# Splitting the fields of a pairwise bilinear kernel: later and spread over the row, with the last subtraction on VectorE

## The chip, the cores and the metric

The kernel runs on one core of a Trainium2 chip. The metric is the device time of one execution in microseconds (us). TensorE is called PE (its weight loads PEld), VectorE DVE, ScalarE ACT, GpSimd POOL and SyncE SP; a "q" behind a name means that engine's instruction queue, from which it also issues transfers.

## The reference

There are 32 fields, a batch of 1024 and an embedding of 128. For each of the 496 pairs of fields (i, j) with i < j, the rows of field i are multiplied by the pair's own 128 x 128 matrix, and the result is multiplied elementwise by field j:

```
v_i = inputs[:, I_IDX, :]
v_j = inputs[:, J_IDX, :]
transformed = jnp.einsum('bpd,ped->bpe', v_i, W)
return transformed * v_j
```

Everything is float32. The output has 1024 x 496 x 128 elements, 260 MB; the inputs are 16.8 MB of fields and 32.5 MB of matrices.

## The kernel before

The pairs are walked row by row: a row is one field i, from 30 down to 0, with j from i + 1 to 31, so row i has 31 - i pairs and the rows become longer toward the end. `pairs` lists them, and `first_q[i]` is the number of row i's first pair. Each pair q has two units u = 2q and 2q + 1, one for each half of the batch (512 columns). The schedule is manual: every engine carries out its instructions in the order in which the Python code issues them.

A pair's product is held in one of four PSUM tiles (`po`). The first 15 pairs (`nq0`) use plain float32 matmuls (L223). From there on the kernel splits each operand into parts that TensorE takes in its fp32r form, and computes a product from three matmuls: `first(u)` issues xh with wh and xl with wl (L226), then ACT scales the PSUM tile (L228); `second(u)`, three units later (`LAG`), adds xd with wd (L237). After a pair's second half DVE multiplies `po` by field j into an output tile `ot` (L247). Four pairs share an output tile of 2 MB, which is stored with one transfer from the ACT queue (L276).

The parts come from two helpers. `split_w(c)` makes wh, wl and wd of two pairs' matrices: one ACT instruction (L136) and three on POOL (L138, L139, L140). `split_x(f, a)` makes the parts of one half of field f, beginning at column a: xh on ACT (L154), xl on POOL (L155 and its scaling L156), and xd, the difference of xh and xl. For fields above NF - 2 - NATIVE - SHARED, which is 9 here, xd is put in the list `later` and issued to DVE up to `XDLAG` = 10 units after the split, but no later than two units past 2 * first_q[f] (L286). For fields 0 to 9 it is a third POOL instruction (L160). The parts of a field lie in `spool`, which has two sets, so field i's set is the one that field i + 2 used.

The calls of both helpers are in the list `todo` with the pair from which each may run and the pair by which it is due. The list is sorted by the due pair. Once per pair (at odd u) the first item that may run is taken, behind the unit's own instructions. A weight split may run five pairs ahead of its due pair, and one becomes free every second pair. The two halves of field i may run from the second pair of row i + 1; since the weight splits that are due earlier go first, they are taken two pairs apart near that row's start.

The matrices come in tiles of eight pairs, 512 KB. `rpool` has three slots for them (`WB` = 3). Odd-numbered tiles from 13 on, and the early tiles, are one transfer on SP (L120), called at a pair that `w_at` lists. Even-numbered tiles from 12 on (`WAPART`) are called when the tile three before has been split completely (for tile 56, tile 54); POOL transfers 112 of their rows (L104) and SP the other 16 (L105), and a small transfer to `mark` follows on POOL a few pairs later (L101). SP carries out its transfers in order, and each waits for its slot to be free. Field 0 has no tile of its own: `load_x(0)`, called at pair 421, takes one of these three slots:

```
if f == 0:
    t = rpool.tile([P, WL, P], F32, tag="w", name="x_0").rearrange("p q e -> p (q e)")
```

The slot is free again when both halves of field 0 have been split. Toward the end, tile 54 is called at pair 409, tile 55 at 429, tile 56 at 433, tile 58 at 441 (when the last split of tile 55 has been issued), tile 57 at 445 and tile 59 at 455. Tile 57's first split is issued at pair 451; the last splits of tiles 55 and 56 at pairs 441 and 449.

Fields 1 to 16 come in four groups of 2 MB (`load_group`, L110) at the pairs of `XAT`. Until a group is loaded its place serves as an output tile, so there are seven output tiles at first, and three from pair 293 on, which is near 440 us.

Of the kernel before, what the change touches and what calls it, by code (L numbers as in the profile page):

```python
# [12 lines left out]
NF = 32  # L13
# [5 lines left out]
OG = 4  # L19
EPS = 2.0**-12  # L20
NATIVE = 5
SHARED = 16
XDLAG = 10
LAG = 3
PB = 4
# [22 lines left out]
def kernel(  # L48
# [99 lines left out]
    def split_x(f, a, u):  # L148

        if a == 0:  # L150
            x_s[f] = [spool.tile([P, BT], F32R, tag=t, name=f"{t}_{f}") for t in ("xh", "xl", "xd")]
        s = slice(a, a + HB)
        h, l, d = [t[:, s] for t in x_s[f]]
        nc.scalar.mul(h, x_sb[f][:, s], 1.0 - 2.0**-13)  # L154
        nc.gpsimd.tensor_tensor(l, x_sb[f][:, s], h.bitcast(F32), ALU.subtract)  # L155
        nc.gpsimd.tensor_scalar(l, l.bitcast(F32), 1.0 / EPS, 1.0, ALU.mult, ALU.mult)  # L156
        if f > NF - 2 - NATIVE - SHARED:
            later.append((min(u + XDLAG, 2 * first_q[f] + LAG - 1), d, h.bitcast(F32), l.bitcast(F32)))
        else:
            nc.gpsimd.tensor_tensor(d, h.bitcast(F32), l.bitcast(F32), ALU.subtract)  # L160
# [3 lines left out]
    first_q = {i: q for q, (i, j) in reversed(list(enumerate(pairs)))}  # L164
# [3 lines left out]
    todo = []  # L168
    for c in range(c0, nchunk):
        todo.append(((c - 3) * WC + 1, max(c * WC, nq0), lambda u, c=c: split_w(c, u)))  # L170
    for i in range(NF - 2 - NATIVE, -1, -1):
        for a in range(0, BT, HB):
            todo.append((first_q[i + 1] + 1 if i < NF - 3 - NATIVE else 2, first_q[i], lambda u, i=i, a=a: split_x(i, a, u)))
    todo.sort(key=lambda t: t[1])

    load_w(0, (0, 1, WL), nc.sync)
# [79 lines left out]
    for u in range(2 * NQ + LAG + SLAG):  # L256
        q = u // 2
        if u < 2 * NQ:
            i, j = pairs[q]
# [60 lines left out]
```

## Time and profile before

| | before |
|---|---|
| runs, median (lowest to highest) | 752.89 us (751.0 to 753.16), three runs |
| profiled execution: own time / span | 754.8 us / 752.9 us |
| mean granted TensorE clock | 0.989 |
| PE / DVE / ACT / POOL busy | 705.0 / 628.6 / 636.3 / 613.4 us |
| read from HBM / written to it | 49.29 MB / 260.05 MB |
| mean rate of the transfers over the span | 412 GB/s |
| xd on DVE (L286) | 32 instructions of 1054 ns |
| xd on POOL (L160) | 20 instructions of 1289 ns |
| xl on POOL (L155, L156) | 52 of about 1300 ns, 52 of 687 ns |
| weight split on POOL (L138, L139, L140) | 241 each of 761, 412 and 740 ns |

The span runs from the first to the last instruction of the profiled execution. The page splits it into 40 slices and gives, for each, how busy the engines and the 16 DMA engines were. The table of waits names, for idle time of an engine, the instruction that waited and the one it waited for. A window is a stretch of the span with the same figures. A line number like L138 is that of the listing above.

### The profile page before, as it was taken

Reading aid. Unit: us, or ns where it says so; the run is one execution under the profiler, and the core shown is the slowest. Engines: PE = TensorE matmul, PEld = TensorE weight load, DVE = VectorE, ACT = ScalarE, POOL = GpSimd, SP = SyncE. Lnnn points to the kernel's source line nnn. Section 1 sums busy time; section 2 is a strip of 40 time slices with the busy share of each in tenths; the row PEclk is TensorE's granted clock in tenths of the full one; section 3 lists DMA queues with packets and bytes.
Section 4 is the critical chain, followed back from the end, with each engine's and each line's share of the span. In section 5 each row is a group of like instructions: output and inputs, shape, how many; then the busy total and the mean of one; then the engine's idle time right before and its main releaser. Section 6 shows DMA issues by size and latency. Waiting matters only on the chain.

```text
span 752.9 us, 10606 instructions
## 1 busy us (share of the span) xinstructions
PE 705.0 (94%) x2946; PEld 551.4 (73%) x2946; DVE 628.6 (83%) x530; ACT 636.3 (85%) x1256; POOL 613.4 (81%) x902
## 2 busy tenths in 40 slices
PE   7999999989999999999999989889999999999994
PEld 3577777777787778777778767668787777777783
DVE  3888999979999999987889878578888888877785
ACT  1298999979999999998899978689999898988893
POOL 1789999988888898898988879678888878797660
PEclk9999999999999999999999999999999999999997
DMA  9999999999999999999999999999999999999988
GB/s 345 423 428 427 428 429 426 430 403 379 411 411 423 426 424 426 423 426 418 422 432 422 425 425 402 424 393 392 422 411 424 396 420 401 416 413 405 420 361 338
DMA packets 32938, 310.03 MB, mean 412 GB/s; under 512 B 5104, under 2 KB 5232, under 8 KB 16752
## 3 DMA queue, kind: packets, MB, share of 16 engines
q10 hardware_dynamic: 19584, 261.10, 82.6%
q1 hardware_dynamic: 8864, 36.77, 12.3%
q0 software_dynamic: 4432, 11.48, 4.2%
q8 instruction: 24, 0.39, 0.2%
q14 instruction: 34, 0.28, 0.1%
HBM read 49.29 MB, written 260.05 MB: 411 GB/s over the span
## 4 chain that ended last, share of the span: by engine, by line
PE 58%; POOL 13%; DMA 13%; DVE 8%; issue 4%; ACT 2%; ACTq 0%; SPq 0%; DVEq 0%; POOLq 0%
PE po L226 37%; PE po L237 18%; DMA out_dram<-ot 10%; DVE ot L247 5%; PE po L223 3%; POOL xl L155 3%; POOL wl L138 3%; POOL xd L160 3%; DMA x_g<-in_xt_dram 2%; DVE xd L286 2%; POOL wd L140 2%; POOL xl L156 1%; ACT po L228 1%; POOL wd L139 1%; DMA x<-in_xt_dram 1%
## 5 line engine op out<-in xcount | busy, mean ns | idle before, releaser
L228 ACT ACTIVATE po<-po 128x512 f32<-128x512 f32 x962 | 554.2, 584 | 81.6 <-PE po L226 66.9
L247 DVE TENSOR_TENSOR ot<-po,x 128x1024 f32<-128x1024 f32 x358 | 432.4, 1222 | 78.3 <-DMA out_dram<-ot 18.3
L226 PE MATMUL po<-xh,wh 128*128 128x512 f32 x962 | 381.0, 396 | 15.5 <-DVE ot L247 14.1
L226 PE MATMUL po<-xl,wl 128*128 128x512 f32 x962 | 377.8, 393 | 13.7 <-POOL wl L138 13.5
L237 PE MATMUL po<-xd,wd 128*128 128x512 f32 x962 | 377.1, 392 | 6.7 <-ACT po L228 3.1
L226 PEld LDWEIGHTS po<-xh,wh 128*128 128x128 f32 x962 | 181.3, 189 | 69.2 <-DVE ot L247 32.2
L138 POOL TENSOR_TENSOR wl<-w,wh 128x256 fp32r<-128x256 f32 x241 | 183.4, 761 | 57.3 <-ACT wh L136 53.1
L226 PEld LDWEIGHTS po<-xl,wl 128*128 128x128 f32 x962 | 181.4, 189 | 55.7 <-POOL wl L138 18.4
L237 PEld LDWEIGHTS po<-xd,wd 128*128 128x128 f32 x962 | 181.3, 189 | 47.5 <-ACT po L228 4.8
L247 DVE TENSOR_TENSOR ot<-po,x_g 128x1024 f32<-128x1024 f32 x136 | 164.9, 1224 | 37.0 <-PE po L237 15.6
L140 POOL TENSOR_TENSOR wd<-wl,wd 128x256 fp32r<-128x256 f32 x241 | 178.3, 740 | 20.1
L139 POOL TENSOR_SCALAR wd<-wh 128x256 fp32r<-128x256 f32 x241 | 99.3, 412 | 20.5
L136 ACT ACTIVATE wh<-w 128x256 fp32r<-128x256 f32 x241 | 98.6, 410 | 7.7 <-DVE ot L247 5.7
L155 POOL TENSOR_TENSOR xl<-x_g,xh 128x512 fp32r<-128x512 f32 x32 | 41.6, 1300 | 2.0 <-ACT xh L154 1.7
L156 POOL TENSOR_SCALAR xl<-xl 128x512 fp32r<-128x512 f32 x52 | 35.7, 687 | 4.6
L155 POOL TENSOR_TENSOR xl<-x,xh 128x512 fp32r<-128x512 f32 x20 | 26.2, 1312 | 15.9 <-ACT xh L154 15.6
L286 DVE TENSOR_TENSOR xd<-xh,xl 128x512 fp32r<-128x512 f32 x32 | 33.7, 1054 | 0.3 <-POOL xl L156 0.3
L223 PE MATMUL po<-x,w 128*128 128x512 f32 x60 | 29.2, 644 | 4.2 <-DMA x<-in_xt_dram 4.2
L160 POOL TENSOR_TENSOR xd<-xh,xl 128x512 fp32r<-128x512 f32 x20 | 25.8, 1289 | 1.7
L223 PEld LDWEIGHTS po<-x,w 128*128 128x128 f32 x60 | 11.9, 204 | 20.7 <-issue 14.6
L154 ACT ACTIVATE xh<-x 128x512 fp32r<-128x512 f32 x20 | 12.3, 624 | 11.6 <-DMA x<-in_xt_dram 11.5
L154 ACT ACTIVATE xh<-x_g 128x512 fp32r<-128x512 f32 x32 | 20.0, 624 | 2.0 <-DMA x_g<-in_xt_dram 2.0
(8 smaller groups left out, 36.5 us busy)
## 6 DMA issues: line engine op xcount, KB each, us to landing
out_dram<-ot ACTq DMA_DIRECT2D x122, 2048.0 KB, 12.7
w<-in_wt_dram SPq DMA_DIRECT2D x36, 512.0 KB, 10.7
w<-in_wt_dram POOLq DMA_DIRECT2D x25, 448.0 KB, 11.6
x_g<-in_xt_dram SPq DMA_DIRECT2D x4, 2048.0 KB, 18.5
x<-in_xt_dram SPq DMA_DIRECT2D x14, 512.0 KB, 9.6
out_dram<-ot ACTq DMA_DIRECT2D x6, 512.0 KB, 8.4
w<-in_wt_dram SPq DMA_DIRECT2D x26, 64.0 KB, 6.2
x<-in_xt_dram ACTq DMA_DIRECT2D x4, 256.0 KB, 5.8
```

The source lines that it names most:

```text
L136: halved[c] = nc.scalar.mul(h, raw, 1.0 - 2.0**-13)
L138: nc.gpsimd.tensor_tensor(l, raw, h.bitcast(F32), ALU.subtract)
L139: nc.gpsimd.tensor_scalar(d, h.bitcast(F32), EPS, 1.0, ALU.mult, ALU.mult)
L140: nc.gpsimd.tensor_tensor(d, l.bitcast(F32), d.bitcast(F32), ALU.subtract)
L155: nc.gpsimd.tensor_tensor(l, x_sb[f][:, s], h.bitcast(F32), ALU.subtract)
L160: nc.gpsimd.tensor_tensor(d, h.bitcast(F32), l.bitcast(F32), ALU.subtract)
L223: nc.tensor.matmul(po[q][:, s], w_raw[q // WL][:, q % WL, :], x_sb[i][:, s], start=True, stop=True)
L226: m = nc.tensor.matmul(po[q][:, s], w_s[c][t][:, r], x_s[i][t][:, s], start=t == 0, stop=t == 1)
L228: scaled[u] = nc.scalar.mul(po[q][:, s], po[q][:, s], 1.0 + EPS)
L237: m = nc.tensor.matmul(po[q][:, s], w_s[q // WC][2][:, r], x_s[i][2][:, s], start=False, stop=True, skip_group_check=True)
L247: taken[q] = nc.vector.tensor_tensor(ots[g][:, k, :], po.pop(q), x_sb[j], ALU.mult)
L286: nc.vector.tensor_tensor(*later.pop(0)[1:], ALU.subtract)
```

## The change

SHARED goes from 16 to 26, so the bound NF - 2 - NATIVE - SHARED goes from 9 to -1, and the xd of every field that is split is issued to DVE. The pair from which the two halves of a field may be split moves: row i + 1 has NF - 2 - i pairs, and the first half may be split from one fifth of the row, the second half from three fifths. The due pairs do not change, nor do the fields 25 and 24, which are split near the kernel's start.

```diff
-SHARED = 16
+SHARED = 26
...
     for i in range(NF - 2 - NATIVE, -1, -1):
         for a in range(0, BT, HB):
-            todo.append((first_q[i + 1] + 1 if i < NF - 3 - NATIVE else 2, first_q[i], lambda u, i=i, a=a: split_x(i, a, u)))
+            at = first_q[i + 1] + (NF - 2 - i) * (1 + 2 * (a > 0)) // 5 + 1 if i < NF - 3 - NATIVE else 2
+            todo.append((at, first_q[i], lambda u, i=i, a=a: split_x(i, a, u)))
```

For field 0, whose preceding row has 30 pairs and begins at pair 435, the halves are split at pairs 442 and 454; before they were split at 436 and 438.

## The prediction

> **What bounds the kernel now.** I read the page's first two parts, then the table of waits, then windows of 10 us, then SP's own waits and the timelines around 675 us. First the page:
>
> ```profile
> PE 705.0 (94%) x2946; PEld 551.4 (73%) x2946; DVE 628.6 (83%) x530; ACT 636.3 (85%) x1256; POOL 613.4 (81%) x902
> ...
> DMA  9999999999999999999999999999999999999988
> GB/s 345 423 428 427 428 429 426 430 403 379 411 411 423 426 424 426 423 426 418 422 432 422 425 425 402 424 393 392 422 411 424 396 420 401 416 413 405 420 361 338
> DMA packets 32938, 310.03 MB, mean 412 GB/s; under 512 B 5104, under 2 KB 5232, under 8 KB 16752
> ```
>
> The transfers bind. They run at 420 to 430 GB/s wherever nothing is amiss, and 310.03 MB at 427 would take 726 us of the 752.9. TensorE is close behind: its matmuls start 0.227 us apart in the timeline near 440 us, so a pair of six costs 1.36 us, while a pair's 512 KB of output and 64 KB of weights cost 0.59 MB / 427 GB/s = 1.38 us. So a stall of an engine costs time only where the transfers run dry behind it, or at the end, where no weights are left to load. The table of waits (microseconds, times, longest) shows both kinds:
>
> ```profile
> DVE ot L247 <- DMA out_dram<-ot: 25.9, 22, 4.2
> PEld po L226 <- POOL wl L138: 18.4, 13, 2.4
> PE po L226 <- DVE ot L247: 14.1, 17, 3.4
> PE po L226 <- POOL wl L138: 13.5, 12, 2.0
> ```
>
> GpSimd's splits stop TensorE 12 times for 13.5 us: by windows of this table, 3.0 us in 130 to 215 us, 4.7 in 320 to 440, 5.8 in 440 to 700, about 1.2 us once in each late row. VectorE waits for stores 25.9 us, 22.8 of it in 440 to 700, where three output tiles are left. Where the transfers do run dry is seen in the windows (busy time and count of each engine, granted clock, DMA share, GB/s):
>
> ```profile
> 130.00:150.00 20.00, 18.97 (x84) 15.17 (x83) 18.35 (x16) 18.16 (x37) 18.46 (x27) 1.00 1.01 428
> 160.00:170.00 10.00, 9.98 (x37) 8.09 (x38) 6.92 (x6) 7.11 (x14) 8.51 (x14) 0.83 0.93 386
> 170.00:180.00 10.00, 10.00 (x46) 8.28 (x45) 9.19 (x9) 9.78 (x21) 8.67 (x13) 1.00 0.97 341
> 500.00:510.00 10.00, 8.84 (x39) 6.89 (x38) 7.50 (x7) 8.54 (x18) 9.38 (x13) 1.00 0.88 368
> 510.00:520.00 10.00, 10.00 (x46) 8.29 (x45) 8.95 (x8) 9.31 (x20) 9.21 (x16) 1.00 1.01 361
> ```
>
> [...] a 512 KB weight transfer lands 10.5 us after its issue in 500 to 712 us, behind queued stores, and after 5.7 us in 165 to 215 us, where stores land in 8.2 instead of 14.0 us (230 to 330 us). [...] here the same subtraction takes 1289 ns on POOL (L160) and 1054 ns on VectorE (L286), so the measured ratio of 1.22 is used. [...]
>
> **The change part by part.** (1) The subtraction xd of fields 0 to 9 leaves POOL: 20 x 1289 ns = 25.8 us. VectorE gains 20 x 1054 ns = 21.1 us, 628.6 + 21.1 = 650 us of 753, two in each of ten rows. In rows 5 to 0 that is 12 x 1.05 = 12.6 us, beside 22.8 us in which VectorE waits for stores. One such store issues up to 1 us late; a store lands about 12.0 us after issue there, some 6 us of it behind the one ahead, so a late store should still find the transfers busy. I take 0; if the cover fails, 12 x (1.05 - 0.9 us, a usual wait for a store in VectorE's timeline after 550 us) is about 2 us and 12.6 the end that nothing supports. No gain is possible from this term alone.
>
> (2) Each field's halves are split at one and three fifths of the preceding row and not two pairs apart at its start. Per two pairs (2.7 us) POOL has one weight split of 761 + 412 + 740 = 1.9 us; a half adds 1300 + 687 (+ 1289) ns = 2.0 (3.3) us, so today two halves in a row put it 1.2 (2.5) us per half behind, and the weight split after them is late. Dealt out, and without xd, one half puts it 1.2 us behind and there are 4 to 12 pairs to recover, so the 13.5 us of stalls on POOL should go, as should ACT's 2.0 us wait for x_g near 350 us. What is late next is the transfers, so this pays only where they ran dry. Against 427 GB/s, 160 to 190 us lost 0.96 + 2.0 + 0.3 = 3.3 us (386, 341 and 413 GB/s): a 2.0 us stall on POOL came just before 160, the clock fell to 0.83 in the first window and few stores were queued. I take 3.0 back. 500 to 520 lost 1.4 + 1.5 us; the one stall of 1.2 us there is taken back, the half-speed clock is not. 580 to 590 (401 GB/s, 0.6 us lost) gives 0.3. Rows 9 to 7 (320 to 440 us) give nothing: a backlog of stores covers their stalls. Sum -4.5 us, bounds -6.5 and -0.5.
>
> (3) In the short rows a clamp holds xd of the second half at two units before the row: VectorE's product 1.22 + xd 1.05 = 2.3 us against the 1.36 us until TensorE wants it, 0.9 us for each of fields 23 to 18, with one xd more for field 23: 6.5 us. PEld and PE waited about 12 us in 36 to 160 us already, on the bursts, and the transfers run at 426 to 430 GB/s there. I take 0 (bounds -1, +1).
>
> (4) **A slot is held longer.** Field 0 lies in one of the three slots of the weights. Its halves are split at pairs 436 and 438 today, at 442 and 454 after. SP's waits in 655 to 680 us show whom the slot goes to:
>
> ```profile
> SPq L120 <- POOL wl L138: 13.2, 2, 8.8
> SPq L105 <- POOL xl L155: 10.9, 1, 10.9
> ```
>
> The second line is weight tile 58 (called at pair 441), which takes field 0's slot when its xl is done; tile 57 (called at 445, first split at 451) is queued behind it on SP and takes tile 55's at 667.72. After the change tile 58 takes tile 55's, field 0 is still in its own, tile 56 is read until pair 449: tile 57 has no slot until the wl of pair 449. ACT runs in order, so its wh for pair 451 blocks all evictions behind it, and TensorE with them. The timelines of ACT and POOL give the events:
>
> ```profile
> 674.38 0.41 ACT L136 ACTIVATE wh<-w 128x256 fp32r<-128x256 f32 x1
> 679.17 0.42 ACT L136 ACTIVATE wh<-w 128x256 fp32r<-128x256 f32 x1 [1.99 <-DMA w<-in_wt_dram]
> ```
>
> ```profile
> 676.30 0.73 POOL L138 TENSOR_TENSOR wl<-w,wh 128x256 fp32r<-128x256 f32 x1
> ```
>
> The wh of 674.38 is that of pair 449. With POOL free its wl ends at 674.4 + 0.4 + 0.8 = 675.6; a weight transfer then lands 10.5 us later (10.3 to 12.0), at 686.1 instead of 679.1. ACT is 6.9 us later than today; today's wait of 2.0 us already reaches TensorE with 0.7, so nothing is left to absorb the rest. By then the stores have drained, so the 2.3 us that TensorE still lost to full tiles after 679 (1.7 of it after 700 us by the waits) disappear, and the rest of the kernel runs at TensorE's pace. Net +4.6 us, bounds 0 and +7.
>
> Sum: -4.5 + 4.6 = +0.1 us. The profiled execution took 754.8 us with a span of 752.9; the median of the runs is 752.89, 1.9 us below it. The difference goes on the median: **753.0 us**.
>
> **The rivals.** (F) Faster: the new slot wait does not bite, because the slots go round otherwise than SP's waits suggest, or the transfer lands early as the stores drain. For it: it rests on one place. Against it: the 10.9 us line and the steady 10.5 us. Then 752.9 - 4.5 = 748.4. (S) Slower: the slot wait of (4) at pair 451, price 4.6 us, decides as soon as part (2) gives back less than 2.3 us, because the slow stretches at 160 and 500 us come from the half clock and from thin queues and not from POOL; then up to 757.5. For it: both stretches follow a drop of the clock, and stalls of the same 1.2 us at 543 and 624 us leave the next store's landing where it was. The 2 us of (1) would add to this side. (N) The dealing is not carried out: one item is taken per odd unit, earliest due first, but weight splits come free only at every other pair, so each half moves by a pair at most; I give this nothing.
>
> **How the numbers follow.** 0.3% is 2.3 us, about what a measurement of this kernel can tell from no change. Forecast, 0.45: own range 750.0 to 755.5, of which 0.06 falls faster, 0.34 within, 0.05 slower. F, 0.30: 0.26 faster, 0.04 within. S, 0.25: 0.24 slower, 0.01 within. That makes 0.32, 0.39 and 0.29. The range 748.0 to 757.5 reaches to both rivals' values; beyond lie S with the cost of (1), and F with all 6.5 us of (2), together under 2 in 10.
>
> **What would show it.** Right: no L160 and 52 of L286; PE's wait on POOL wl under 3 us; no window of 160 to 190 us under 400 GB/s; one ACT wait of about 8 to 9 us on DMA w near 680 us, a dry stretch of transfers after it, and no wait on stores from there to the end. Wrong: no such ACT wait (F); 160 to 180 us as slow as before (S); VectorE's waits for stores gone after 440 us and PE waiting for ot in their place, which would be the cost of (1).

## The result, and the profile after

The change makes the kernel slower: 759.56 us median (758.67 to 761.63, four runs) against 751.94 (750.99 to 753.16, four runs), a ratio of 1.0104 with a 95% interval of 1.0076 to 1.0133. That is 7.6 us more, where no change was forecast. The two profiled executions took 758.67 and 754.8 us, so before's is 2.9 us above its own median: the traces are read here for what happens, the ratios for how much.

Line numbers are one higher after the changed line (L227 is the old L226). First the page of the changed kernel:

```profile
PE 703.2 (93%) x2946; PEld 554.7 (73%) x2946; DVE 636.3 (84%) x550; ACT 632.5 (84%) x1256; POOL 594.3 (79%) x882
...
DMA  9999999999999999999999999999999999997998
GB/s 345 427 424 404 383 427 428 379 400 431 410 414 415 426 422 426 425 423 427 425 423 424 426 423 365 428 424 423 425 419 426 420 419 426 405 406 276 401 427 337
DMA packets 32939, 310.04 MB, mean 410 GB/s; under 512 B 5104, under 2 KB 5232, under 8 KB 16752
```

The work has moved as told: POOL is down 19 us, and VectorE is up 8 us: its xd is now 52 instructions of 867 ns, where it was 32 of 1054. The rate of the transfers has new dips: slices 4 and 5, 8 and 9 (which begin at 57 and at 132 us), and 276 GB/s in the slice that begins at 681 us. A fourth, 365 in slice 25, stands where a wait of 5.8 us for full output tiles has just ended. It is no sign of the loss: two kernels below that are not slower than before, SHARED 26 alone and the one with the short rows put back, show 371 there. The old dip of slice 10 (379) is gone, and so are those of slices 27 and 28 (393 and 392). The table of waits:

```profile
DVE ot L248 <- DMA out_dram<-ot: 25.6, 16, 6.6
PE po L227 <- DVE ot L248: 17.7, 12, 5.8
PE po L238 <- ACT po L229: 9.4, 3, 7.6
PEld po L227 <- POOL xl L156: 7.6, 5, 3.1
PE po L227 <- POOL xl L156: 5.7, 4, 2.7
PE po L238 <- DVE xd L287: 5.8, 5, 1.5
```

TensorE's waits on the weights' wl (13.5 us before) are gone. Waits on a field's xl and xd have grown to 11.5 us together (1.4 before), and there is one of 7.6 us on ACT. Its waits for ot are fewer and longer: twelve of up to 5.8 us instead of seventeen of up to 3.4. The windows of the changed kernel show the first two new dips:

```profile
60.00:70.00 10.00, 10.00 (x45) 8.00 (x43) 9.28 (x9) 9.78 (x20) 8.74 (x12) 1.00 0.98 412
70.00:80.00 10.00, 8.70 (x39) 7.14 (x39) 8.62 (x9) 8.51 (x18) 9.16 (x15) 1.00 0.95 371
80.00:90.00 10.00, 7.86 (x34) 5.88 (x33) 7.94 (x8) 7.25 (x16) 8.25 (x12) 1.00 1.00 364
130.00:140.00 10.00, 8.47 (x37) 6.42 (x36) 9.03 (x8) 7.81 (x17) 9.20 (x14) 1.00 0.98 387
140.00:150.00 10.00, 10.00 (x45) 8.26 (x45) 9.19 (x9) 9.78 (x21) 8.96 (x12) 1.00 0.97 366
```

Before, these five windows moved 424 to 431 GB/s. The third dip is the slot. SP's waits in 650 to 700 us, then the timelines of POOL and ACT:

```profile
SPq L105 <- POOL wl L138: 22.3, 3, 9.8
SPq L120 <- POOL xl L155: 16.8, 1, 16.8
SPq L120 <- POOL wl L138: 10.2, 1, 10.2
```

```profile
673.61 0.73 POOL L138 TENSOR_TENSOR wl<-w,wh 128x256 fp32r<-128x256 f32 x1
```

```profile
672.88 0.41 ACT L136 ACTIVATE wh<-w 128x256 fp32r<-128x256 f32 x1
685.03 0.42 ACT L136 ACTIVATE wh<-w 128x256 fp32r<-128x256 f32 x1 [8.63 <-DMA w<-in_wt_dram]
```

It is now a later weight tile, 59, that waits for field 0's xl (the second line). Tile 57 is the third line: SP issues it at 674.37, just as the wl of 673.61 ends, and it lands about 10.6 us later. ACT stands still for 8.63 us. The wh of 672.88 is that of pair 449, which stood at 674.38 before. So up to this point the traced execution of the changed kernel is 1.5 us ahead, and it ends 4.0 us behind (spans of 756.9 and 752.9 us): between these two executions 5.5 us are lost from here on.

### The profile page after: what moved, and what is told of

The parts are those of the page before. It is cut to its first block, busy times and chain, and to the rows that moved or that the text cites. A ratio compares the mean times of both kernels' runs of the same rounds, so it can differ in the third digit from the quotient of the medians.

```text
span 756.9 us, 10630 instructions
## 1 busy us (share of the span) xinstructions
PE 703.2 (93%) x2946; PEld 554.7 (73%) x2946; DVE 636.3 (84%) x550; ACT 632.5 (84%) x1256; POOL 594.3 (79%) x882
## 4 chain that ended last, share of the span: by engine, by line
PE 76%; DMA 13%; DVE 4%; POOL 3%; issue 2%; ACT 1%; ACTq 0%; DVEq 0%; POOLq 0%
PE po L227 48%; PE po L238 24%; DMA out_dram<-ot 11%; PE po L224 4%; DVE ot L248 3%; DMA w<-in_wt_dram 1%; ACT po L229 1%; DVE xd L287 1%; POOL xl L155 1%; POOL wd L140 1%; DMA x<-in_xt_dram 1%; POOL wl L138 1%; POOL wd L139 0%; POOL xl L156 0%; DVE ot L246 0%
## 5 line engine op out<-in xcount | busy, mean ns | idle before, releaser
L227 PE MATMUL po<-xh,wh 128*128 128x512 f32 x962 | 382.1, 397 | 18.0 <-DVE ot L248 17.7
L227 PE MATMUL po<-xl,wl 128*128 128x512 f32 x962 | 378.1, 393 | 5.7 <-POOL xl L156 5.7
L227 PEld LDWEIGHTS po<-xh,wh 128*128 128x128 f32 x962 | 182.4, 190 | 68.4 <-DVE ot L248 30.5
L227 PEld LDWEIGHTS po<-xl,wl 128*128 128x128 f32 x962 | 182.5, 190 | 44.2 <-POOL xl L156 7.6
L140 POOL TENSOR_TENSOR wd<-wl,wd 128x256 fp32r<-128x256 f32 x241 | 180.6, 749 | 20.1
L139 POOL TENSOR_SCALAR wd<-wh 128x256 fp32r<-128x256 f32 x241 | 102.2, 424 | 20.5
L287 DVE TENSOR_TENSOR xd<-xh,xl 128x512 fp32r<-128x512 f32 x52 | 45.0, 867 | 0.0
L156 POOL TENSOR_SCALAR xl<-xl 128x512 fp32r<-128x512 f32 x52 | 33.1, 636 | 4.6
L154 ACT ACTIVATE xh<-x 128x512 fp32r<-128x512 f32 x20 | 12.3, 625 | 11.5 <-DMA x<-in_xt_dram 11.3
L101 POOL DMA_DIRECT2D mark<-in_xt_dram x26 | 16.6, 637 | 0.0
## 6 DMA issues: line engine op xcount, KB each, us to landing
w<-in_wt_dram POOLq DMA_DIRECT2D x25, 448.0 KB, 11.6
```

What stands on the lines that cost most here:

```text
L139: nc.gpsimd.tensor_scalar(d, h.bitcast(F32), EPS, 1.0, ALU.mult, ALU.mult)
L140: nc.gpsimd.tensor_tensor(d, l.bitcast(F32), d.bitcast(F32), ALU.subtract)
L227: m = nc.tensor.matmul(po[q][:, s], w_s[c][t][:, r], x_s[i][t][:, s], start=t == 0, stop=t == 1)
L287: nc.vector.tensor_tensor(*later.pop(0)[1:], ALU.subtract)
```

## The experiments

Twelve kernels ran in three groups of four, each group against its own runs of the kernel before on the same chip (medians 752.72, 752.27 and 751.10 us; the second group ran on another chip than the other two). Ratios are to those, with the 95% interval in brackets. In the diffs, `D` stands for the change's formula and `E` for the old `first_q[i + 1] + 1`.

**Field 0 put back in the changed kernel.**

```diff
-at = D if i < NF - 3 - NATIVE else 2
+at = (D if i > 0 else E) if i < NF - 3 - NATIVE else 2
```

> The change whole, but field 0 is split at pairs 436 and 438 as before, so weight tile 57 has its slot as before. The change costs 7.6 us by the medians (759.56 against 751.94). Slot theory (tile 57's late slot stops ACT and TensorE): ACT's wait on the weight transfer near 676 us falls from 8.6 to about 2 us and the time falls by 5 to 7 us, to 752.5 to 754.5. Rival, early rows (the second halves of fields 23 to 18 come too late, the transfers run dry in 60 to 160 us and the clock drops): it falls by under 3 us, to 756.5 or more. Rival, xd on VectorE: the same, 756.5 or more.

It took 757.04 us, a ratio of 1.0063 (1.0043 to 1.0083). ACT's wait fell to 1.5 us, but the time by only 0.4% of the kernel, as the rivals and not the slot theory expected. The slot is part of the loss; the rest lies elsewhere.

**Field 0 alone dealt out in the kernel before.**

```diff
-at = E if i < NF - 3 - NATIVE else 2
+at = (D if i == 0 else E) if i < NF - 3 - NATIVE else 2
```

> The kernel before with field 0 alone dealt out (pairs 442 and 454), SHARED 16. Slot theory: 4 to 6 us slower than before (756 to 758), with a wait of 8 to 9 us of ACT on the weight transfer near 677 us and TensorE idle for about 7.6 us. Rivals: within 1.5 us of before, since neither the short rows nor VectorE's xd change.

It took 759.32 us, 1.0109 (1.0072 to 1.0146): the slot by itself costs about 8 us here by the ratio, more than expected. ACT waited 10.2 us for the tile and TensorE 8.6.

**SHARED 26 alone.**

```diff
-SHARED = 16
+SHARED = 26
```

> SHARED 26 alone: xd of all fields on VectorE, halves at the old pairs. Slot theory and early rows: within 2 us of before (750 to 754), since neither is touched; TensorE's waits on POOL wl fall from 13.5 to some 5 us. Rival, xd on VectorE costs the late rows: 3 us or more slower than before (755 or more), with TensorE waiting on ot in rows 5 to 0.

It took 751.22 us, 0.9992 (0.9972 to 1.0011). TensorE's waits on POOL wl fell to 3.0 us and those on ot rose from 14.1 to 20.4 us, and nothing was gained or lost: the rival that VectorE's xd costs the late rows 3 us or more falls. Ending the stalls of the late rows, by itself, is worth nothing that can be measured.

**The dealing alone.** The changed kernel with SHARED 16.

> The dealing alone, SHARED 16: fields 0 to 9 keep xd on POOL. Slot theory plus early rows: as slow as the whole change, 757 to 761, with the ACT wait of 8 to 9 us and the dry stretch of 60 to 90 us. If xd on VectorE carries the loss: 753 or less.

It took 762.01 us, 1.0134 (1.0096 to 1.0172), a little more than expected, with ACT's wait of 9.1 us and transfers at 369 to 373 GB/s in 70 to 90 us. The dealing carries the loss. The interval overlaps that of the whole change, so whether VectorE's xd gives something back here isn't settled by it.

**Short rows put back.** Only fields 17 to 1 are dealt out, with SHARED 26.

```diff
+at = (D if 0 < i < 18 else E) if i < NF - 3 - NATIVE else 2
```

> Dealing only for fields 17 to 1; fields 25 to 18 and field 0 as before, xd of all fields on VectorE. The kernel with field 0 alone put back took 757.04 us, before 752.72, SHARED 26 alone 751.22. Short-rows theory (late second halves of fields 23 to 18 empty the transfers in 60 to 160 us): 750.5 to 752.5, and no window of 60 to 160 us under 420 GB/s. Rival, long rows (TensorE running ahead to full output tiles, long waits, clock at half afterwards): 755 or more.

It took 748.04 us, 0.9944 (0.9917 to 0.9971): faster than before, and better than expected. The page's rates show no dip in the first slices after the start:

```profile
GB/s 347 424 424 428 429 429 427 428 424 424 427 414 423 426 424 423 428 422 423 426 426 427 422 429 371 425 426 424 424 423 425 421 424 424 417 409 415 423 379 342
```

The slices that cover 160 to 200 us, which fell to 379 GB/s before, move 424 or more.

**Short rows alone.** The kernel before, with fields 23 to 18 dealt out (`D if i >= 18 else E`).

> The kernel before with the dealing for fields 23 to 18 alone, SHARED 16, field 0 as before. Short-rows theory: 3 to 5 us slower than before (755.5 to 758). Rival, long rows: within 1.5 us of before.

It took 757.82 us, 1.0077 (1.0047 to 1.0107): the short rows cost some 5.8 us by themselves, by the ratio.

**Tile 57 ahead of tile 58.** The change whole, with field 0 held until pair 454, but tile 58 is called when tile 56 has been split (pair 449), so that tile 57 takes tile 55's slot.

```diff
-if w_next and (XAFTER if w_next[0] == XAFTER + 2 else w_next[0] - WB) in spent:
+if w_next and (w_next[0] - 2 if w_next[0] in (XAFTER + 2, XAFTER + 4) else w_next[0] - WB) in spent:
```

> The change whole, with weight tile 58 called when tile 56 has been split (pair 449) instead of tile 55 (441), so that tile 57, called at 445, takes tile 55's slot at once while field 0 still holds its own. Slot theory: ACT waits 2 us or less for tile 57 and the time is that of the kernel with field 0 put back (757.0, between 755 and 758.5). Rival, it is the late split of field 0 and not the slot: 759 or more.

It took 755.27 us, 1.0032 (1.0014 to 1.0049), with ACT's wait at 1.1 us, as the slot theory expected. Field 0 is split as late as in the change, so it is the slot and not the late split. The share of the slot within the whole change is thus 1.04 - 0.63 = 0.4% by the first experiment and 1.04 - 0.32 = 0.7% by this one, each give or take 0.35; by itself it costs 1.1%. Why the two differ by 0.3% is open.

**TensorE kept busy during the wait.** The kernel with field 0 alone dealt out has 34 more matmuls, whose products are overwritten:

```diff
+if u == 2 * 453 + 1:
+    for _ in range(34):
+        m = nc.tensor.matmul(po[q][:, s], w_s[c][0][:, r], x_s[i][0][:, s], start=True, stop=True)
+        apart(m, scaled.get(u - 1))
```

> The kernel before with field 0 alone dealt out (759.32 us), and 34 more matmuls issued ahead of the second half of pair 453, whose products are overwritten: at 0.22 us each they fill about 7.4 of the 8.6 us in which TensorE stands still for tile 57. Clock theory (half speed follows TensorE's idle time): no half-speed stretch at 680 to 690 us, where it was 10.2 us long with 4.2 us of it after the restart, and 1.5 to 2.5 us faster, 757 to 758. Rival, the half speed has another cause: the stretch stays, and the time is the same or longer, 759.3 to 762.

It took 755.70 us, 1.0048 (1.0029 to 1.0067), against 1.0109 without them, which ran in the first group. Adding 7.4 us of useless matmuls saves 0.6% (0.2 to 1.0), 4.6 us by the ratios and 3.6 by the medians. No half-speed stretch is left at 680 to 690 us, as the clock theory expected, and the gain is larger than it expected. ACT still waits 8.7 us in this trace; it waited 10.2 in the one without, so a part of the difference between the traces can be the shorter wait. Windows of the kernel without them (TensorE's busy time and count first, granted clock, DMA share and rate last):

```profile
680.00:686.00 6.00, 0.00 (x0) 0.00 (x0) 0.00 (x0) 0.94 (x3) 0.48 (x1) 0.50 0.12 48
686.00:690.00 4.00, 3.92 (x9) 3.14 (x10) 1.23 (x1) 3.35 (x7) 3.17 (x6) 0.50 0.47 197
```

and of the kernel with them:

```profile
680.00:686.00 6.00, 6.00 (x28) 4.70 (x27) 0.05 (x1) 2.24 (x5) 1.64 (x3) 1.00 0.31 127
686.00:690.00 4.00, 4.00 (x19) 3.23 (x18) 3.62 (x3) 3.94 (x9) 3.36 (x5) 1.00 0.93 393
```

Without them TensorE restarts at half clock and does 9 matmuls in 4 us instead of 19. The granted clock is 0.50 from 680 to 690 us there, and 1.00 over the same 10 us in the kernel with them.

**Both losses taken out.** Fields 17 to 0 are dealt out (`D if i < 18 else E`), tile 57 comes first, and SHARED is 26.

> Both found losses taken out of the change: dealing for fields 17 to 0 only, and weight tile 57 ahead of tile 58; xd of all fields on VectorE. With field 0 at its old pairs this took 748.04 us, 0.56% under before. Theory (short rows and the slot are the whole loss): 0.3 to 0.8% under before, 746 to 750 us. Rival (dealing field 0 costs something beside the slot): over 751.

It took 747.41 us, 0.9942 (0.9920 to 0.9964): faster than both kernels, and within what was expected if the short rows and the slot are the whole loss.

**The same with SHARED 16.**

> The same with SHARED 16, so that fields 0 to 9 keep xd on GpSimd. If dealing alone ends the late rows' stalls and VectorE's part is worth nothing: within 1 us of the kernel with SHARED 26, 747 to 750. If moving xd matters once the halves are dealt: 1.5 us or more above it, with waits of TensorE on POOL wl in rows 9 to 0.

It took 747.45 us, 0.9946 (0.9918 to 0.9974): the same. TensorE's waits on POOL wl in 320 to 700 us, before and then here:

```profile
PE po L226 <- POOL wl L138: 10.5, 10, 1.2
```

```profile
PE po L227 <- POOL wl L138: 0.5, 1, 0.5
```

Dealing alone ends the stalls of the late rows. With the halves dealt, no difference is measured between the two engines for xd (to about 0.35%).

**Field 23 alone, and fields 22 to 18 alone,** dealt out in the kernel before (`D if i == 23 else E`, `D if 18 <= i < 23 else E`).

> The kernel before with field 23 alone dealt out (its halves at pairs 24 and 26, row 23 begins at pair 28). The fields 23 to 18 together cost 0.77%, 5.8 us. If the first stop carries it (2.7 us without matmuls at 51 us, then 3.4 us at half speed): 2.5 to 4.5 us slower than before, with the half-speed stretch at 53 us. If the five later rows carry it: under 1.5 us slower.

> The kernel before with fields 22 to 18 alone dealt out, field 23 as before. If the first stop of field 23 and its half-speed stretch carry the loss of the short rows: under 2 us slower than before. If stops of about 1 us on xl and xd in each of these rows carry it: 3 us or more slower, and transfers under 400 GB/s in 130 to 160 us.

They took 755.62 us, 1.0062 (1.0042 to 1.0082), and 754.22 us, 1.0032 (1.0013 to 1.0051). Both expectations hold in part: field 23 costs 0.6% and the five others 0.3%; dealt out together they cost 0.8%, which within the intervals is the sum. Windows of the kernel with field 23 alone:

```profile
53.00:57.00 4.00, 1.88 (x7) 1.24 (x7) 0.90 (x2) 1.66 (x4) 3.67 (x6) 1.00 1.00 424
57.00:60.00 3.00, 1.29 (x5) 0.82 (x6) 2.50 (x3) 1.41 (x3) 1.94 (x4) 1.00 0.97 414
60.00:70.00 10.00, 10.00 (x39) 8.05 (x38) 7.52 (x7) 8.04 (x18) 7.52 (x11) 0.83 0.78 329
70.00:80.00 10.00, 8.71 (x39) 6.92 (x38) 8.78 (x9) 8.20 (x18) 8.86 (x12) 1.00 0.96 365
80.00:90.00 10.00, 9.84 (x43) 7.63 (x42) 9.71 (x10) 9.62 (x21) 9.33 (x13) 1.00 1.00 351
```

TensorE starts 12 matmuls in these 7 us, where at 0.227 us from one to the next it has room for 31. The half-speed stretch follows, at 60 us and not at 53 as expected; the transfers drop at the same time and stay low for 30 us. Fields 22 to 18 have their dip later: 397, 395 and 379 GB/s in 130 to 160 us, as expected.

## Why the prediction was wrong, point by point

**Part (1), xd on VectorE, taken at 0: nothing measured speaks against it.** SHARED 26 alone gave -0.08% (-0.28 to +0.11). That run ends the stalls of the late rows as well, for which part (2) took 1.5 us, so the 2 us named for a failing cover are not excluded by it. With the halves dealt, xd on VectorE or on POOL gave 0.9942 and 0.9946.

**Part (2), dealing ends the stalls, taken at -4.5 us: right in size, the source of the gain is open.** In the long rows, where only this part acts, the dealing gave -0.54% without and -0.58% with VectorE's xd, -3.7 us each by the medians, and the stalls on POOL wl are gone. But SHARED 26 alone ends all of them except the early ones and gains nothing. For 160 to 190 us the part took 3.0 us back, from one trace in which the clock fell to half after the stop of 2.02 us on POOL wl. The trace of SHARED 26 alone has the same stop, 2.00 us long, at full clock, and its transfers moved 419, 416 and 406 GB/s there, not 386, 341 and 413. So between these two traces most of that dip goes with the half clock, as rival S said, and not every trace has it.

**Part (3), the short rows, taken at 0 with bounds of 1 us: this step failed.** By itself it measured +5.8 us. Within the change it is more: the kernel with tile 57 first (1.0032) and the one that also has its short rows put back (0.9942) lie 0.9% apart, 6.8 us; with field 0 at its old pairs it is 1.2% (1.0063 and 0.9944), each give or take 0.3. The clamp on xd was seen: TensorE waits 5.8 us on xd. Three things were not. First, the second half's xl is late too. Field 23's is issued two pairs before row 23, and in the changed kernel TensorE stops 2.67 us for it, then again for other fields. Second, the step set against its 6.5 us some 12 us of waits of PEld and PE that were there already. Of those in the table for 36 to 160 us, the matmuls' own are the ones that stop TensorE, and they are few:

```profile
PE po L237 <- DVE xd L286: 1.2, 1, 1.2
PE po L237 <- ACT po L228: 1.2, 1, 1.2
PE po L226 <- DVE ot L247: 1.1, 2, 0.6
PE po L226 <- POOL wl L138: 1.0, 1, 1.0
PE po L226 <- POOL xl L156: 0.2, 1, 0.2
```

That is 4.7 us; the others are waits of weight loads, which overlap the matmuls (551.4 us of weight loads and 705.0 us of matmuls in a span of 752.9). In the changed kernel the matmuls wait 11.6 us there: 5.8 on xd, 0.9 on ACT, and

```profile
PE po L227 <- POOL xl L156: 4.9, 3, 2.7
```

Third, the cover did not hold. The step took a rate of 427 GB/s as proof that stores were queued and a late engine cost nothing. The landing times of stores issued in 55 to 95 us, before and then after, show how much was queued:

```profile
out_dram<-ot ACTq DMA_DIRECT2D x6, 2048.0 KB, 12.9
out_dram<-ot ACTq DMA_DIRECT2D x6, 2048.0 KB, 8.4
```

The difference of 4.5 us is about one store of 2 MB at 427 GB/s (4.9 us), so by this estimate one store was in reserve, and the added stops used it up. Over 44 to 160 us the transfers moved 405 GB/s instead of 428, a shortfall worth 6.2 us. The runs show which fields cost the time; that it went through the emptied queue is read from the traces, and how much of it is the half clock after the first stop is open.

**Part (4), the slot, taken at +4.6 us: right in mechanism, and within the change in size.** The events came as told: no slot for tile 57 until the wl of pair 449, a landing time of 10.6 us, ACT's wait of 8.6 us, TensorE's of 7.6, ACT 5.9 us later than before, and almost no waits for stores from there on (1.8 us from 655 us to the end). That it is 5.9 and not 6.9 us comes mostly from the wl, which ended at 674.3 us and not at 675.6. Within the change the slot measured 0.4 to 0.7%, 3 to 5 us. By itself it measured +8.2 us, of which keeping TensorE busy removed about 4.6, by the ratios. What the sum left out is in "the rest of the kernel runs at TensorE's pace": after the stop that pace is half for some microseconds (in the changed kernel 7 matmuls in 686 to 689 us at a granted clock of 0.51, and 14 in the next 3 us at 1.00).

So the sum had +0.1 us, and the 7.5 us that it lacks are about what the short rows cost within the change. The four parts measured alone come to -0.08 - 0.54 + 0.77 + 1.09 = +1.2%, give or take 0.6, and the whole is 1.04%.

The rivals: F fell, since the wait is there. S named part (4) as the decider if part (2) gave back too little; part (2) gave back what was expected, so S's sign was right for a reason that was not its own. N fell: the second half of field 23 came late enough to stop TensorE. The marks set for the profile were met at the slot and at 160 us, and missed the dip at 60 to 90 us, for which none had been set.

## What to carry to other kernels

Work that is dealt out by a share of the time before it must still keep a fixed lead in the shortest stretch: here three fifths of a row of seven pairs left two pairs, 2.7 us, while xh, xl and xd of one half take 0.6, 2.0 and 0.9 us one after the other. Moving the last reader of a tile moves the release of its slot (tile 57 was issued at 667.72 us before and at 674.37 after), so look up who takes that slot next, on which queue, and what waits behind it in order. A rate of 427 GB/s did not tell how much work was queued behind it; by the estimate above the time from a store's issue to its landing did, 12.9 us before and 8.4 after.

## What the runs showed of the hardware

A stop of TensorE can slow the matmuls behind it. The timeline of the changed kernel, start and duration first:

```profile
53.85 0.65 PE L227 MATMUL po<-xl,wl 128*128 128x512 f32 x1 [2.67 <-POOL xl L156]
54.30 0.63 PE L238 MATMUL po<-xd,wd 128*128 128x512 f32 x1
54.73 0.63 PE L227 MATMUL po<-xh,wh 128*128 128x512 f32 x1
...
59.00 0.40 PE L238 MATMUL po<-xd,wd 128*128 128x512 f32 x1
59.23 0.40 PE L227 MATMUL po<-xh,wh 128*128 128x512 f32 x1
```

After the stop of 2.67 us the matmuls start 0.43 us apart, and by 59 us 0.23 again; the granted clock is 0.57 in 54 to 58 us and 1.00 in the 4 us after. Not each stop does it: one of 2.56 us at 442 us in the kernel before left the clock at full. Windows of the kernel before, around its stops of 2.02 and 2.56 us (length, then TensorE's busy time; the granted clock is the third number from the end):

```profile
156.73:160.14 3.41, 1.39 (x7) 0.85 (x6) 2.33 (x3) 1.94 (x4) 3.16 (x4) 1.00 0.99 421
160.14:163.55 3.41, 3.41 (x9) 2.64 (x10) 1.23 (x1) 1.39 (x3) 3.16 (x6) 0.50 0.99 414
440.03:443.45 3.42, 2.35 (x11) 1.62 (x9) 0.22 (x1) 2.94 (x7) 3.17 (x6) 1.00 1.02 422
443.45:446.86 3.41, 1.91 (x8) 1.60 (x9) 3.19 (x3) 0.97 (x2) 1.64 (x3) 1.00 1.01 428
446.86:450.27 3.41, 3.41 (x16) 2.81 (x16) 2.34 (x3) 3.16 (x7) 1.27 (x3) 1.00 1.02 435
```

and in the kernel with SHARED 26 alone, around the stop of 2.00 us:

```profile
154.66:158.08 3.42, 2.43 (x11) 1.69 (x9) 3.10 (x4) 3.06 (x7) 3.25 (x4) 1.00 1.06 449
158.08:161.49 3.41, 2.40 (x10) 1.99 (x11) 1.83 (x3) 1.62 (x3) 3.16 (x5) 1.00 0.99 420
161.49:164.90 3.41, 3.41 (x16) 2.82 (x15) 3.13 (x3) 3.04 (x7) 3.16 (x6) 1.00 0.97 393
```

Behind the stop of 2.02 us the granted clock is 0.50 for 3.41 us, with 9 matmuls in them; behind those of 2.56 and 2.00 us it stays at 1.00, with 16 matmuls in as long a time. So the length of a stop does not decide it alone: the longest of these three left the clock at full. What else does is not shown, nor why the kernel with field 23 alone has its half-speed stretch at 60 us (granted clock 0.83 over 60 to 70 us, 1.00 over 53 to 60) and not right behind its stop of 2.7 us. Keeping TensorE at work on products that are thrown away was worth 0.6% of the kernel (0.2 to 1.0) where it would have stood still for 8.6 us.
